# A graph network's third layer on TensorE: products by halves in its first block, and who mixes the features for them

## The chip, the cores and the metric

The kernel runs on one core of a Trainium2 chip. A core has five engines with an instruction queue each: TensorE (PE in the profile; its loading of weights is PEld), VectorE (DVE), ScalarE (ACT), GpSimd (POOL) and SyncE (SP, which here only starts DMAs). An engine takes its instructions in order and waits for semaphores of the others. The metric is the device time of one execution in microseconds; lower is better. Before the change it is 2798.02 us, the median of three runs (2794.73 to 2802.38).

## The reference

Four graph layers on 4096 nodes with 256 features; each adds its result to its input and normalises the rows. What matters here is the third layer (and the end of the second, whose last block is finished while the third begins):

```
def _L2_gnn_ref(x, adj, W, a):
    h = x @ W
    e_src = h @ a[:D, 0]
    e_dst = h @ a[D:, 0]
    e = e_src[:, None] + e_dst[None, :]
    e = jnp.where(e > 0, e, NEG_SLOPE * e)
    att_logits = jnp.where(adj > 0, e, MASK_VAL)
    attention = jax.nn.softmax(att_logits, axis=1)
    h_prime = attention @ h
    return jax.nn.elu(h_prime)
...
x = _layernorm(x + _L1_gnn_ref(x, adj, ...), axis=-1)
x = _layernorm(x + _L2_gnn_ref(x, adj, L2_gnn_W, L2_gnn_a), axis=-1)
```

All of it is float32.

## The kernel before

`additive_one` computes the third layer. The 4096 target nodes are taken in 8 blocks of 512 (`b`), the 4096 source nodes in 32 tiles of 128, two tiles to a pair (`g`, 16 pairs in a block). So there are 128 units (b, g). For each unit `weights(b, g)` makes the unnormalised attention weights: ScalarE an activation per tile into a PSUM bank (line 566, tile `r`, two banks), VectorE one operation per tile (line 567) that adds a term and multiplies by the mask, which SyncE loads (line 554, four buffers). The result is `prob`, 128 sources x 2 tiles x 512 targets. `sums(b, g)` multiplies it by the features of the sources, X, and adds up over all pairs in PSUM; W is applied afterwards, to the sums (`project`).

A pair can be multiplied in two ways. Plainly: four matmuls of 128 x 128 features with 512 targets (line 581), two banks in use. Or by Strassen's scheme on the 2 x 2 halves (two tiles, two halves of the features, two halves of the targets): seven products with 256 targets (`product`, line 446) in place of eight, on four banks `acc0` to `acc3`. The seven need sums and differences of the operands. Those of the weights, `mix`, come anew for each unit (`mix_weights`: line 436 on VectorE, 512 columns; lines 437 and 438 on GpSimd, 256 columns each). Those of the features, `mixed`, are made once for the layer, by `mix_features` for a group `q` of two pairs at a time (eight groups; four operations on lines 429 to 432). Before the change block 0 is multiplied plainly throughout, while VectorE makes the mixed features of all groups after each second pair; blocks 1 to 7 use the seven products. At the end of a block the four banks are combined into the four quarters of the result (`first_half`, `second_half`: lines 451 to 460); in block 0 three copies do (lines 589 to 591).

The order of the work is written out by hand for TensorE, VectorE and ScalarE: a loop over the units, in which `weights` runs three units ahead of `sums` (`LAG`). GpSimd and SyncE are ordered by a scheduler, within what the program fixes. In block 0 the loop also takes the steps of the second layer's tail (`next(before, None)`, with a number of steps for some pairs): it adds up the row sums `den` (line 867), row sums and transposes on TensorE (lines 880, 888, 895), divides and adds to X (909, 912), takes statistics (156, 157), the root (161 to 171, of which 168 to 171 and the lifting of the mean, 190 and 191, on GpSimd), scales the last four tiles of rows (186) and takes their dot products (504); then `factors` (511 to 513). Only after that can the weights of the last two pairs, 14 and 15, be made: their sources are these rows. `first_mask` holds the masks of pairs 0 and 1.

Of the kernel before, what the change touches and what calls it, by code (L numbers as in the profile page):

```python
# [9 lines left out]
FP = mybir.dt.float32  # L10
# [18 lines left out]
def kernel(  # L29
# [395 lines left out]

    def mix_features(t, q):

        x = X[:, 4 * q:4 * q + 4, :D].rearrange("p (g n) (h f) -> p g n h f", n=2, h=2)
        nc.vector.tensor_tensor(t[:, :, 0, :], x[:, :, 0, 1, :], x[:, :, 0, 0, :], OP.subtract)
        nc.vector.tensor_tensor(t[:, :, 1, :], x[:, :, 1, 1, :], t[:, :, 0, :], OP.add)  # L430
        nc.vector.scalar_tensor_tensor(t[:, :, 2, :], x[:, :, 1, 1, :], -1.0, x[:, :, 0, 1, :], OP.mult, OP.subtract)
        nc.vector.tensor_tensor(t[:, :, 3, :], x[:, :, 1, 0, :], t[:, :, 1, :], OP.subtract)

    def mix_weights(s, z, eng):

        nc.vector.tensor_tensor(s[:, :2, :], z[:, 0, :].rearrange("p (h i) -> p h i", h=2), z[:, :, HW:], OP.subtract)  # L436
        eng.tensor_tensor(s[:, 2, :], z[:, 0, :HW], s[:, 1, :], OP.subtract)
        eng.tensor_tensor(s[:, 3, :], z[:, 1, :HW], s[:, 2, :], OP.subtract)

    def product(acc, z, s, t, g, n):  # L440
# [5 lines left out]
        nc.tensor.matmul(acc[at][:, half * HW:(half + 1) * HW], w, a, start=(g == 0 and half == 0),  # L446
                         stop=(g == NP - 1), skip_group_check=True)

    def first_half(c, one, acc):
# [17 lines left out]
    class Additive:  # L467
# [38 lines left out]

        def factors(self, b):

            t = slice(b * QB, (b + 1) * QB)
            d = self.dot[:, t, 1]  # L510
            nc.scalar.activation(self.dst[:, t], d, AF.Exp)
            nc.scalar.activation(self.own[:, t], d, AF.Exp, scale=self.slope)
            nc.vector.tensor_scalar_mul(self.less[:, t], self.own[:, t], -1.0)

# [12 lines left out]
    def additive_one(w_sb, ga, tail, op, follow):  # L527

        with ExitStack() as lay:
# [13 lines left out]
            edges = adjT.rearrange("(t p) i -> p t i", p=P)  # L543
            mixed, acc, prob, mix, mvs, roots, kept, drawn, ys, far_y = {}, {}, {}, {}, {}, {}, {}, {}, {}, {}

            def bank():
                return ps.tile([P, QW], FP, name="g")

            def weights(b, g):
# [13 lines left out]
                for n in range(2):  # L563
# [3 lines left out]
                    nc.vector.scalar_tensor_tensor(z[:, n, :], r, ga.own[:, j:j + 1], mask[:, n, :], OP.add, OP.mult)  # L567
                if b:
                    s = mix[b, g] = zp.tile([P, 4, HW], FP, name="mix")
                    mix_weights(s, z, nc.gpsimd)  # L570

            def sums(b, g):
                if g == 0:
                    acc[b] = [pa.tile([P, QW], FP, name=f"acc{n}") for n in range(4)]
                if b:
                    for n in range(7):
                        product(acc[b], prob[b, g], mix[b, g], mixed[g // 2][:, g % 2], g, n)
                else:
                    for j in range(2 * g, 2 * g + 2):
                        for c in range(KC):  # L580
                            nc.tensor.matmul(acc[b][c], X[:, j, c * P:(c + 1) * P], prob[b, g][:, j % 2, :],
                                             start=(j == 0), stop=(j == NT - 1))
                if g == NP - 1:
                    c = kept[b] = op.tile([P, 4, HW], FP, name="quarters")
                    if b:
                        first_half(c, op.tile([P, HW], FP, name="one"), acc[b])
                        second_half(c, acc[b])
                    else:
                        nc.scalar.copy(c[:, :2, :], acc[b][0].rearrange("p (h i) -> p h i", h=2))
                        nc.vector.tensor_copy(c[:, 3, :], acc[b][1][:, :HW])  # L590
                        nc.vector.tensor_copy(c[:, 2, :], acc[b][1][:, HW:])

# [54 lines left out]
            fixed = {mybir.EngineType.PE, mybir.EngineType.DVE, mybir.EngineType.Activation}  # L647
            before = tail(bank)
            with tc.manual_schedule(engines=fixed):
                for i in range(len(units) + LAG):  # L650
                    b, g = units[i - LAG] if i >= LAG else (-1, 0)
                    if g == NP - 1:
                        sums(b, g)
                    if i < len(units):
                        weights(*units[i])
                    if b >= 0:
# [4 lines left out]
                        else:  # L661
                            for _ in range({4: 3, 6: 2, 7: 3, 8: 4, 9: 3, 10: 4}.get(g, 0)):
                                next(before, None)
                            if g == 11:
                                follow.start()
                            elif g == 14:
                                follow.centre(bank())
                            if g % 2:
                                t = mixed[g // 2] = keep.tile([P, 2, 4, P], FP, name=f"mixed{g // 2}")
                                mix_features(t, g // 2)  # L670
                        if b > 2 and g == 0:
# [19 lines left out]
    def multi_head_attention(w_sb, b_sb, tail, rows_of_den, rows_done, narrow_edges, ga):  # L691
# [290 lines left out]
        def tail(bank):  # L982
# [19 lines left out]
            yield  # L1002
            end_root(v, r, n, nc.gpsimd)
            lift_mean(mv, v, r, nc.gpsimd)
            yield
            for k in range(QB):
                scale_row(X[:, b * QB + k, :D], mv, r, k)
                ga.dots(b * QB + k, (1,))
                yield
            ga.factors(b)  # L1010
            rows_done()
# [375 lines left out]
```

## Time and profile before

| | us |
|---|---|
| median of three runs | 2798.02 |
| lowest and highest run | 2794.73, 2802.38 |
| the profiled execution: its own time | 2795.6 |
| its span in the profile | 2793.8 |
| block 0 of the third layer on TensorE | 1713.81 to 1772.03 |
| blocks 1 to 7 and the fourth layer | the rest, to 2793.8 |

The granted clock of TensorE is 1.0 in the profiled execution. In the profile, a line of the timeline gives the start, the length, the engine, the line of the kernel, what is written and read, how many instructions were merged, and in brackets how long the engine had been idle before and for whom it waited. A group of instructions gives its busy time, the mean duration in ns, and the idle time before it. Matmuls and weight loads have two records each. TensorE's matmuls overlap, so the pace is read from start to start.

### The profile page before, as it was taken

The page shows a single profiled execution, that of the slowest core. Times are in us where ns is not written, and L with a number is a line of the kernel's source. Part 1 is how long each engine was busy: PE and PEld are TensorE (multiplying, and loading weights), DVE is VectorE, ACT ScalarE, POOL GpSimd, SP SyncE. Part 2 cuts the span into 40 slices and gives each one's busy share as a digit, 9 for nine tenths or more (in the row PEclk, how much of TensorE's full clock was granted, in tenths as well). Part 3 has the DMA queues.
Part 4 walks back from the last instruction along what each step waited for, and adds up shares of the span by engine and source line. Part 5 has one row for each costly group of instructions (what it writes and reads, how often), then busy time and mean ns, then how long its engine had stood idle before and what let it go on. Part 6 is the DMA issues. An engine that isn't in the chain of part 4 may idle for free. (4 is left out here: it accounts for less than half of the span.)

```text
span 2793.8 us, 50176 instructions
## 1 busy us (share of the span) xinstructions
PE 2774.1 (99%) x19445; PEld 1427.4 (51%) x19445; DVE 2289.0 (82%) x3040; ACT 1700.7 (61%) x2650; POOL 1052.5 (38%) x986
## 2 busy tenths in 40 slices
PE   9999999999999999999999999999999999999999
PEld 5333333333453333333333333788888777777776
DVE  8899999999677788887888878888887877767676
ACT  7899999999336666666666666465556422222222
POOL 0000100100029878778788793345455000000000
PEclk9999999999999999999999999999999999999999
DMA  7566676665339899998988988567778545445442
GB/s 206 107 142 137 139 144 130 137 143 114 70 97 191 186 178 196 191 188 182 197 182 189 192 181 187 168 198 207 183 207 232 121 76 82 74 71 82 75 72 44
DMA packets 275065, 411.92 MB, mean 147 GB/s; under 512 B 54809, under 2 KB 155657, under 8 KB 273930
## 3 DMA queue, kind: packets, MB, share of 16 engines
q0 software_dynamic: 104176, 182.74, 41.3%
q1 hardware_dynamic: 164280, 218.88, 26.7%
q10 hardware_dynamic: 6370, 7.10, 0.7%
q8 instruction: 152, 2.49, 0.4%
q14 instruction: 87, 0.71, 0.1%
HBM read 335.94 MB, written 39.40 MB: 134 GB/s over the span
## 5 line engine op out<-in xcount | busy, mean ns | idle before, releaser
L834 DVE TENSOR_TENSOR prob<-p,mask 128x1024 f32<-128x1024 f32 x512 | 620.0, 1222 | 166.9 <-ACT p L824 159.9
L824 ACT ACTIVATE p<-p,shift 128x1024 f32<-128x1024 f32 x512 | 557.0, 1090 | 317.8 <-PE p L822 317.1
L312 PE MATMUL acc<-prob,V 128*32 128x512 f32 x6144 | 664.0, 592 | 1.2 <-DVE prob L302 1.2
L299 ACT ACTIVATE prob<-row,dst 128x512 f32<-128x512 f32 x1020 | 635.9, 716 | 0.4
L302 DVE SCALAR_TENSOR_TENSOR prob<-prob,mask 128x2048 f32<-128x2048 f32 x256 | 580.6, 2288 | 25.8 <-ACT prob L299 24.8
L844 POOL TENSOR_TENSOR den<-den,prob 128x1024 f32<-128x1024 f32 x220 | 559.8, 2544 | 92.6 <-DVE prob L834 87.2
L822 PE MATMUL p<-qT,kT 64*64 64x512 f32 x4096 | 531.1, 590 | 2.0 <-DVE prob L834 2.0
L858 PE MATMUL acc<-prob,V 64*64 64x512 f32 x4096 | 529.9, 589 | 0.0
L312 PEld LDWEIGHTS acc<-prob,V 128*32 128x32 f32 x6144 | 197.3, 110 | 453.0 <-issue 432.2
L446 PE MATMUL acc<-mix,mixed 128*128 128x256 f32 x1428 | 388.0, 380 | 2.7 <-DVE quarters L460 1.2
L858 PEld LDWEIGHTS acc<-prob,V 64*64 64x64 f32 x4096 | 157.4, 133 | 282.1 <-issue 280.3
L822 PEld LDWEIGHTS p<-qT,kT 64*64 64x64 f32 x4096 | 154.3, 133 | 278.9 <-issue 256.5
L446 PEld LDWEIGHTS acc<-mix,mixed 128*128 128x128 f32 x1428 | 269.5, 190 | 45.0 <-PE acc L446 3.5
L90 POOL COPY tick<-prob 128x1 f32<-128x1 f32 x35 | 38.0, 1086 | 643.0 <-DVE prob L302 642.1
L1130 DVE TENSOR_TENSOR prob<-prob,mask 128x1024 f32<-128x1024 f32 x128 | 156.2, 1220 | 140.5 <-ACT prob L1122 140.1
L850 POOL DMA_DIRECT2D den<-prob x240 | 232.0, 967 | 61.0 <-DVE prob L834 22.3
L446 PE MATMUL acc<-prob,X 128*128 128x256 f32 x952 | 245.7, 380 | 3.4 <-DVE quarters L452 3.3
L1050 POOL DMA_DIRECT2D mask<-in_adjT x64 | 47.7, 745 | 530.1 <-DVE prob L1130 437.6
L446 PEld LDWEIGHTS acc<-prob,X 128*128 128x128 f32 x952 | 180.1, 190 | 84.1 <-issue 56.7
L567 DVE SCALAR_TENSOR_TENSOR prob<-r,own,mask 128x512 f32<-128x512 f32 x252 | 177.1, 744 | 51.3 <-POOL s L169 13.7
L1122 ACT ACTIVATE prob<-p 128x512 f32<-128x512 f32 x144 | 86.1, 598 | 204.1 <-PE p L1118 202.6
L1122 ACT ACTIVATE prob<-g 128x512 f32<-128x512 f32 x112 | 67.0, 598 | 208.7 <-PE g L1118 208.7
(233 smaller groups left out, 2823.1 us busy)
## 6 DMA issues: line engine op xcount, KB each, us to landing
mask<-in_adjT SPq DMA_DIRECT2D x254, 512.0 KB
den<-prob POOLq DMA_DIRECT2D x240, 512.0 KB, 5.3
mask<-edges SPq DMA_DIRECT2D x512, 64.0 KB
mask<-in_adjT POOLq DMA_DIRECT2D x64, 512.0 KB, 5.7
edges<-in_adj POOLq DMA_DIRECT2D x32, 512.0 KB, 9.6
far<-squares SPq DMA_DIRECT2D x16, 512.0 KB
den<-prob SPq DMA_DIRECT2D x16, 512.0 KB
row<-far SPq DMA_DIRECT2D x7, 1024.0 KB
```

Of the source, the lines that this page charges most:

```text
L299: nc.scalar.activation(z[:, h, :], r, AF.Relu, bias=-1.0, scale=dst[:, j, h:h + 1])
L302: nc.vector.scalar_tensor_tensor(z, z, 1.0, mask[m][:, j % MJ, :].unsqueeze(1).to_broadcast([P, H, QW]), OP.add, OP.mult)
L312: nc.tensor.matmul(acc[b][h * G:(h + 1) * G, n, :], part, prob[b, j][:, h, :], start=(j == 0), stop=(j == NT - 1))
L446: nc.tensor.matmul(acc[at][:, half * HW:(half + 1) * HW], w, a, start=(g == 0 and half == 0), stop=(g == NP - 1), skip_group_check=True)
L567: nc.vector.scalar_tensor_tensor(z[:, n, :], r, ga.own[:, j:j + 1], mask[:, n, :], OP.add, OP.mult)
L822: nc.tensor.matmul(p[c * d:(c + 1) * d, r, :], kT[half, c, at:at + d], qT[half, c, cols], start=True, stop=True)
L824: nc.scalar.activation(p, p, AF.Exp, bias=shift)
L834: nc.vector.tensor_tensor(z, p, mask[m][:, j % MJ, :].unsqueeze(1).to_broadcast([P, KC, QW]), OP.mult)
L844: nc.gpsimd.tensor_tensor(to, to, flat, OP.add)
L850: nc.gpsimd.dma_start(to, flat, accum_op=OP.add)
L858: nc.tensor.matmul(acc[b][c][r * d:(r + 1) * d, :], V[half, j, r * d:(r + 1) * d], prob[b, j][half, r, :], start=(j == 0), stop=(j == NH - 1))
L1130: nc.vector.tensor_tensor(z, z, co.mask[b, 2 * g // MJ][:, lo:lo + 2, :], OP.mult)
```

## The change

In block 0, pairs 4 to 13 (`apart`) are now multiplied by the seven products, and pairs 0 to 3, 14 and 15 by eight plain products of 256 targets onto the same four banks (`plain`), so that the end of the block combines the banks as in the other blocks; what the plain products put into the second half of `acc3` is copied apart and added at last (`more`). The mixed features are made earlier and in another order: groups 0, 1 and 2 on VectorE, groups 3 to 7 on GpSimd, but for one operation of each group, which stays on VectorE. The table `mixing` says at which step each group is made. From step 16 on a group's mixing is placed after the last operation that `weights` gave to GpSimd (`last`). The small operations of the tail's root and mean go from GpSimd to VectorE, the multiplication by -1 in `factors` (`less`) from VectorE to ScalarE, and one step of the tail comes a little earlier.

```diff
-    def mix_features(t, q):
+    def mix_features(t, q, eng=nc.vector):
         x = X[:, 4 * q:4 * q + 4, :D].rearrange("p (g n) (h f) -> p g n h f", n=2, h=2)
-        nc.vector.tensor_tensor(t[:, :, 0, :], x[:, :, 0, 1, :], x[:, :, 0, 0, :], OP.subtract)
-        nc.vector.tensor_tensor(t[:, :, 1, :], x[:, :, 1, 1, :], t[:, :, 0, :], OP.add)
+        eng.tensor_tensor(t[:, :, 0, :], x[:, :, 0, 1, :], x[:, :, 0, 0, :], OP.subtract)
+        eng.tensor_tensor(t[:, :, 1, :], x[:, :, 1, 1, :], t[:, :, 0, :], OP.add)
         nc.vector.scalar_tensor_tensor(t[:, :, 2, :], x[:, :, 1, 1, :], -1.0, x[:, :, 0, 1, :], OP.mult, OP.subtract)
-        nc.vector.tensor_tensor(t[:, :, 3, :], x[:, :, 1, 0, :], t[:, :, 1, :], OP.subtract)
+        eng.tensor_tensor(t[:, :, 3, :], x[:, :, 1, 0, :], t[:, :, 1, :], OP.subtract)
...
+    def plain(acc, z, g):
+        for at, to, f, lo in ((0, 0, 0, 0), (1, 1, 1, 0), (2, 1, 0, HW), (3, 1, 1, HW)):
+            for n in range(2):
+                nc.tensor.matmul(acc[at][:, to * HW:(to + 1) * HW], X[:, 2 * g + n, f * P:(f + 1) * P],
+                                 z[:, n, lo:lo + HW], start=(g == 0 and n == 0), stop=(g == NP - 1),
+                                 skip_group_check=True)
...
-        def factors(self, b):
+        def factors(self, b, times=nc.vector.tensor_scalar_mul):
...
-            nc.vector.tensor_scalar_mul(self.less[:, t], self.own[:, t], -1.0)
+            times(self.less[:, t], self.own[:, t], -1.0)
...
+            apart = range(4, 14)
+            mixing = {1: ((2, nc.vector),), 2: ((3, nc.gpsimd), (4, nc.gpsimd)), 3: ((5, nc.gpsimd),),
+                      4: ((0, nc.vector), (6, nc.gpsimd)), 14: ((1, nc.vector),), 16: ((7, nc.gpsimd),)}
...
-                if b:
+                if b or g in apart:
                     s = mix[b, g] = zp.tile([P, 4, HW], FP, name="mix")
-                    mix_weights(s, z, nc.gpsimd)
+                    return mix_weights(s, z, nc.gpsimd)
...
-                if b:
+                if (b, g) in mix:
                     for n in range(7):
                         product(acc[b], prob[b, g], mix[b, g], mixed[g // 2][:, g % 2], g, n)
                 else:
-                    for j in range(2 * g, 2 * g + 2):
-                        for c in range(KC):
-                            nc.tensor.matmul(acc[b][c], X[:, j, c * P:(c + 1) * P], prob[b, g][:, j % 2, :],
-                                             start=(j == 0), stop=(j == NT - 1))
+                    plain(acc[b], prob[b, g], g)
                 if g == NP - 1:
                     c = kept[b] = op.tile([P, 4, HW], FP, name="quarters")
-                    if b:
-                        first_half(c, op.tile([P, HW], FP, name="one"), acc[b])
-                        second_half(c, acc[b])
-                    else:
-                        nc.scalar.copy(c[:, :2, :], acc[b][0].rearrange("p (h i) -> p h i", h=2))
-                        nc.vector.tensor_copy(c[:, 3, :], acc[b][1][:, :HW])
-                        nc.vector.tensor_copy(c[:, 2, :], acc[b][1][:, HW:])
+                    if b == 0:
+                        more = fin1.tile([P, QW], FP, name=f"kept{KC}")[:, :HW]
+                        nc.scalar.copy(more, acc[b][3][:, HW:])
+                    one = op.tile([P, HW], FP, name="one")
+                    first_half(c, one, acc[b])
+                    second_half(c, acc[b])
+                    if b == 0:
+                        nc.vector.tensor_tensor(c[:, 2, :], c[:, 2, :], more, OP.add)
...
+                    for q, eng in mixing.get(i, ()):
+                        t = mixed[q] = keep.tile([P, 2, 4, P], FP, name=f"mixed{q}")
+                        with tc.issue_after(getattr(last, "ins", last)) if i >= NP else nullcontext():
+                            mix_features(t, q, eng)
                     if i < len(units):
-                        weights(*units[i])
+                        last = weights(*units[i]) or last
...
-                            for _ in range({4: 3, 6: 2, 7: 3, 8: 4, 9: 3, 10: 4}.get(g, 0)):
+                            for _ in range({4: 3, 6: 2, 7: 3, 8: 5, 9: 3, 10: 3}.get(g, 0)):
...
-                            if g % 2:
-                                t = mixed[g // 2] = keep.tile([P, 2, 4, P], FP, name=f"mixed{g // 2}")
-                                mix_features(t, g // 2)
...
-            end_root(v, r, n, nc.gpsimd)
-            lift_mean(mv, v, r, nc.gpsimd)
+            end_root(v, r, n)
+            lift_mean(mv, v, r)
...
-            ga.factors(b)
+            ga.factors(b, nc.scalar.mul)
```

## The prediction

> **What bounds the kernel now.** I read the page first, for the engine that sets the end, then the stage of the change: the third layer's first block, about 1713.8 to 1772.0 us. The page's first part:
>
> ```profile
> PE 2774.1 (99%) x19445; PEld 1427.4 (51%) x19445; DVE 2289.0 (82%) x3040; ACT 1700.7 (61%) x2650; POOL 1052.5 (38%) x986
> ```
>
> The view of busy time in a stretch (its length, then each engine's busy time, TensorE's clock, the DMA share and GB/s):
>
> ```profile
> 1713.00:1773.00 60.00, 59.97 (x173) 27.40 (x166) 48.67 (x105) 29.39 (x46) 4.52 (x10) 1.00 0.68 189
> ```
>
> TensorE has no gap, so fewer products save time as long as nothing else is late. VectorE is busy for 48.67 of 60 us; GpSimd is almost idle. The groups of this stage:
>
> ```profile
> L581 PE MATMUL acc<-prob,X 128*128 128x512 f32 x128 | 55.8, 594 | 0.0
> L567 DVE SCALAR_TENSOR_TENSOR prob<-r,own,mask 128x512 f32<-128x512 f32 x36 | 25.5, 746 | 5.7 <-DMA mask<-in_adjT 4.3 <-ACT r L566 1.0
> ...
> L432 DVE TENSOR_TENSOR mixed<-X,mixed 128x256 f32<-128x256 f32 x8 | 3.3, 416 | 0.0
> ...
> L437 POOL TENSOR_TENSOR mix<-prob,mix 128x256 f32<-128x256 f32 x3 | 2.3, 782 | 18.8 <-PE g L1041 14.2 <-DVE mix L436 4.6
> ...
> L436 DVE TENSOR_TENSOR mix<-prob 128x512 f32<-128x512 f32 x3 | 2.1, 692 | 0.1
> ```
>
> The trace holds two records for each matmul, so x128 is 64 matmuls. Next the timelines, for pace and for who is late. TensorE, at the block's end and in the next block:
>
> ```profile
> 1743.69 24.20 PE L581 MATMUL acc<-prob,X 128*128 128x512 f32 x56
> 1767.73 1.03 PE L1041 MATMUL g<-w_sb,ones 128*128 128x256 f32 x4
> 1768.59 3.60 PE L581 MATMUL acc<-prob,X 128*128 128x512 f32 x8
> 1772.03 1.03 PE L446 MATMUL acc<-prob,X 128*128 128x256 f32 x4
> ...
> 1774.55 0.67 PE L446 MATMUL acc<-mix,mixed 128*128 128x256 f32 x2 [1.07 <-DVE quarters L591]
> ```
>
> VectorE's holes in the stage, and two of its operations that ran beside GpSimd's L437 and L438:
>
> ```profile
> 1724.62 1.41 DVE L567 SCALAR_TENSOR_TENSOR prob<-r,own,mask 128x512 f32<-128x512 f32 x2 [3.90 <-DMA mask<-in_adjT]
> ...
> 1754.58 0.41 DVE L186 TENSOR_SCALAR X<-X,mv,r 128x256 f32<-128x256 f32 x1 [2.25 <-POOL mv L191]
> ...
> 1762.02 1.46 DVE L567 SCALAR_TENSOR_TENSOR prob<-r,own,mask 128x512 f32<-128x512 f32 x2 [0.85 <-ACT r L566]
> ...
> 1769.00 0.83 DVE L430 TENSOR_TENSOR mixed<-X,mixed 128x256 f32<-128x256 f32 x1
> 1769.75 0.94 DVE L431 SCALAR_TENSOR_TENSOR mixed<-X 128x256 f32<-128x256 f32 x1
> ```
>
> Two things to see. The weights of pair 14 are written from 1762.02 to about 1763.4, and TensorE reaches pair 14 near 1764.4 (1767.73 less one pair of 3.45): only 1.0 us of slack, because pair 14 uses rows that the second layer's tail finishes in this very stage. And L430 and L431, 0.42 us alone, took 0.83 and 0.94 us while GpSimd worked.
>
> **What the Trainium skill says.** "SBUF — State Buffer", section "SBUF: two separate sides": a VectorE operation with two SBUF inputs and a GpSimd operation that reads SBUF exclude each other for the whole instruction, the later one waits. The two doubled rows agree; L567 (one input in PSUM) stays at 0.74 beside GpSimd. "GPSIMD Engine Reference", section "8. Key points": elementwise work is about twice as fast on VectorE; here 0.73 to 0.78 us against 0.42 for 256 columns.
>
> **The change part by part,** against the profiled execution (span 2793.8, run 2795.6 us).
>
> TensorE. A pair of four 512-column matmuls takes 24.04/7 = 3.43 us in the second stretch and 24.23/7 = 3.46 in the first, 3.45 in the mean. In the next block three pairs of seven products go from 1807.03 to 1816.09: 3.02 each, 0.431 a product. Ten pairs save 10 x 0.43 = 4.3 us. The six plain pairs become eight products of 256, 8 x 0.431 = 3.45: nothing. Freed of all waits, pair 14 would start at 1759.9 and the block end at 1767.7.
>
> VectorE. Added: ten L436 (0.61 us from start to start, 6.1) and six small operations of the tail's root and mean, which leave GpSimd (0.16 each and a dependence, 0.19: 1.1). Removed: of the 24 mixing operations of this stage 7 (the four operations for each of six groups of two pairs become four for groups 0 to 2 and one for groups 3 to 7; 0.36 each, 2.5) and `less`, to ScalarE (0.2). Net +4.5 us: about 53.2 of a stage that wants to shrink to 55.7, so VectorE nearly fills it. I walk its new order, with 2.05 us for a pair with L436 (1781.16 to 1783.21 in the next block) and 0.35 for a dot product:
> - Pairs 0 to 3: the mixing of group 2 (1.46) falls into the 1.67 us before pair 1; the single operations of groups 3 to 6 and all of group 0 (1.4 + 1.46 = 2.9) fall into the 3.90 us before the mask of pair 4. Pair 4 is ready at 1726.0, as before. If all these alternate with GpSimd's twelve mixing operations, at some 0.8 us each, 0.8 later.
> - Pairs 5 to 7 with dots: mix of 4 at 1726.6, + 3 x 2.40, + 2.45 for the two sums of den = 1736.3. TensorE wants den at 1727.65 + 3 x 3.02 = 1736.7. With contention (GpSimd gets in between the two 1.2 us sums, 0.7, and the 0.8 of the start) 1737.5 to 1737.8: TensorE waits about 1.
> - Pairs 8 to 10: 6.2 and 0.5 for ScalarE behind the row sums, 1743.0; halves 3.1, 1746.1 (1745.95 before, so the earlier transposes win nothing); pair 11 2.05; four statistics 2.15; `v` at 1750.3.
> - ScalarE's root 0.5, and the activation of pair 12 now queued behind it 0.8, with hand-offs 1.5 idle; pair 12 2.05; six small operations 1.1; two rows scaled and dotted 1.6; pair 13 2.05; two rows more 1.6: 1760.3. Before: 1760.6.
> - Factors 0.6, activation 0.8, two L567: pair 14 ready at 1763.2. The mixing of group 1 is covered by these 1.4 us; where it alternates with GpSimd's group 7 it lasts some 3 instead of 1.46 and adds 1.5.
> So the chain through the tail is as long as before, and TensorE, ahead by 4.3, runs into it. Its first matmuls of pair 14 start with the first half of pair 14, 1762.7; + 3.75 for the pair, 0.86 for the centring product, 3.46 = 1770.8, a gain of 1.25 on 1772.03. With contention everywhere (0.8 + 0.3 + 1.5) 1773.3, a loss of 1.25.
>
> Moved mixing on GpSimd: 15 operations of 0.73 plus twenty of the weights, 25.6 us in an engine with 4.5 busy; its DMA issues are over at 1714.8. The last two of pair 4's weights end 1728.3 to 1729.2; TensorE wants them at 1728.5 and 1729.4: hidden, with 0.2 to spare.
>
> The change of blocks. Before, the first pair of the next block takes 1772.03 to 1776.35, 4.32, which is 1.30 over 3.02. After, two copies of 0.35 on ScalarE stand before VectorE's chain (at the next boundary 1824.74, 1825.52, 1825.98, 1826.50, 1827.22: 2.9 us), and the third bank is free at its end: 1.6 to 1.8 over. +0.35. SyncE: one weight load goes before a mask, read 20 us later: nothing. Groups 6 and 7 leave the next block's VectorE, which has slack there: nothing.
>
> Sum: -1.25 to +1.25, +0.35: -0.9 to +1.6, middle +0.35. The runs' median is 2798.02, 2.4 above the profiled run, so 2798.3.
>
> **Rivals.**
> - All the gain arrives: -4.3 + 0.35, 2794.1. For it: TensorE is full and GpSimd free. Against: pair 14 would have to be ready by 1759.9, over 3 us earlier than in the walk.
> - Slower: the shared read stretches VectorE's chain. Place: from the den sums to pair 14. Price: each two-input operation that meets GpSimd +0.4; 4 dots behind the weights of pairs 12 and 13 (1.6), L436 in three pairs (0.8), on top of 1.25: +3.7 with the boundary, 2801.7. It decides once the last dot product of the tail ends after about 1761.5. For it: 0.83 and 0.94. Against: in the next block most L436 are at 0.69, since GpSimd is done by then.
>
> **How the numbers follow.** Forecast 0.55, full gain 0.17, slower 0.28. Single runs of before lie from 2794.73 to 2802.38, so each case gets some 2.5 us either side: 2792 to 2804 holds eight in ten. 0.3% (8.4 us) is about what a measurement tells from no change; even the full gain is half of it. Faster by more 0.05, slower by more 0.09 (some stall that I do not see), within it 0.86.
>
> **What would show it.** Right: seven products at 3.02 a pair, then a TensorE gap at pair 14 (and 13) put down to VectorE's prob; VectorE with hardly a hole from 1726 on; mixing operations of 0.8 to 0.9 beside GpSimd. Wrong: no gap at pairs 12 to 14 (then full gain), or gaps on `mix` of GpSimd in every pair (then a loss beyond mine).

## The result, and the profile after

| | before | after |
|---|---|---|
| median of six runs each (us) | 2795.84 | 2807.45 |
| lowest and highest run | 2794.73, 2802.38 | 2802.79, 2809.19 |
| the profiled execution: its own time, its span | 2795.6, 2793.8 | 2802.79, 2801.0 |
| mean granted clock of TensorE in it | 1.000 | 0.998 |

The kernel before has three runs more here than ahead of the change. The ratio after to before is 1.0036, 95% interval 1.0027 to 1.0046, which is some 10 us; the medians lie 11.6 us apart. The forecast was 2798.3 with a range of 2792 to 2804. The time lies outside the range, on the slow side; to a slowing by more than 0.3% the prediction had given 0.09.

Line numbers have moved: the weights are now L578 (L567 before), the activations L577, the plain products L453 (L581 before), den sums L877, reciprocals L913, dot products L512. The mixing of features keeps L429 to L432, the sums of the weights L436 to L438. The page's first part of the changed kernel:

```profile
PE 2773.3 (99%) x19553; PEld 1450.0 (52%) x19553; DVE 2302.6 (82%) x3044; ACT 1697.6 (61%) x2652; POOL 1077.5 (38%) x1015
```

Nothing is to be seen there. The shares are those of before to a per cent, because the stage is 2% of the span. The same 60 us that the prediction looked at, in the view of busy time in a stretch (length, then PE, PEld, DVE, ACT, POOL, TensorE's clock, DMA share, GB/s):

```profile
1713.00:1773.00 60.00, 49.31 (x231) 41.20 (x231) 56.42 (x99) 23.82 (x39) 26.60 (x35) 0.92 0.60 154
```

TensorE, with no gap before, now stands idle for 10.7 of the 60 us, and its mean clock is 0.92; VectorE went from 48.67 to 56.42. The timeline of all engines at the start of the block shows the greater part of it at one place:

```profile
1711.32 1.05 POOL L860 DMA_DIRECT2D den<-prob  x1
1711.42 3.32 PEld L453 LDWEIGHTS acc<-prob,X 128*128 128x128 f32 x16 [0.81 <-issue]
1711.42 3.72 PE L453 MATMUL acc<-prob,X 128*128 128x256 f32 x16
...
1711.58 9.25 DVE L429 TENSOR_TENSOR mixed<-X 128x256 f32<-128x256 f32 x1
1711.91 1.89 POOL L429 TENSOR_TENSOR mixed<-X 128x256 f32<-128x256 f32 x2
...
1718.74 1.80 POOL L432 TENSOR_TENSOR mixed<-X,mixed 128x256 f32<-128x256 f32 x2
1720.86 0.42 DVE L430 TENSOR_TENSOR mixed<-X,mixed 128x256 f32<-128x256 f32 x1
...
1721.88 1.40 DVE L578 SCALAR_TENSOR_TENSOR prob<-r,own,first_mask 128x512 f32<-128x512 f32 x2
```

VectorE's first mixing operation, 0.42 us alone, lasts 9.25 us. It starts at 1711.58, while GpSimd still issues a DMA (1711.32 to 1712.37 by its record, which runs on beside the next operation). From 1711.91 GpSimd goes through its twelve mixing operations without a pause, one about every 0.68 us, to 1720.54; VectorE's operation ends 0.3 us after that. The next one is back at 0.42. Behind it, in the same queue, stand the weights of pair 1, which TensorE wanted at 1714.9 and gets at 1722.67. TensorE's timeline, all of its gaps up to the second block:

```profile
1722.67 12.28 PE L453 MATMUL acc<-prob,X 128*128 128x256 f32 x48 [7.53 <-DVE prob L578]
1765.94 1.13 PE L446 MATMUL acc<-mix,mixed 128*128 128x256 f32 x4 [0.61 <-POOL mix L437]
1770.88 5.16 PE L453 MATMUL acc<-prob,X 128*128 128x256 f32 x16 [2.51 <-DVE prob L578]
1781.10 1.42 PE L446 MATMUL acc<-prob,X 128*128 128x256 f32 x4 [0.74 <-ACT one L459]
```

And the clock after two of these gaps, in the view of stretches:

```profile
1715.00:1722.60 7.60, 0.14 (x1) 0.00 (x0) 7.57 (x6) 0.00 (x0) 5.54 (x9) 0.78 0.87 232
1722.60:1725.00 2.40, 2.33 (x6) 1.83 (x7) 2.40 (x6) 1.84 (x3) 0.00 (x0) 0.50 0.04 7
1725.00:1728.00 3.00, 3.00 (x13) 2.59 (x12) 2.97 (x8) 2.61 (x4) 0.00 (x0) 0.83 0.53 139
...
1771.00:1776.00 5.00, 5.00 (x17) 4.13 (x18) 4.72 (x8) 4.32 (x6) 0.33 (x1) 0.72 0.54 163
```

After the long gap TensorE works at half its clock for over 2 us. Pairs 1 to 3 take 12.12 us (1722.67 to 1734.79) instead of 3 x 3.45 = 10.35.

From the start of block 0 to the second pair of the next block: before 1713.81 to 1776.35, 62.54 us; after 1711.42 to 1785.01, 73.59. The 11.05 more are made up so: ten pairs of seven products -4.3; the gap ahead of pair 1 +7.8; the clock in pairs 1 to 3 +1.8; pair 13 +0.9 (0.61 of it the gap); the gap ahead of pair 14 +2.6; pair 14 at the lowered clock +1.55; change of blocks +0.5: +10.9. (The profiled execution of after is the fastest of its six, its block 0 happens to begin 2.4 us earlier than the one of before, and what follows is 1.5 us shorter, so the spans are only 7.2 apart.)

### The profile page after: what moved, and what is told of

Same layout as the page of the kernel before. It is cut to its first block, busy times and chain, and to the rows that moved or that the text cites. A ratio compares the mean times of both kernels' runs of the same rounds, so it can differ in the third digit from the quotient of the medians.

```text
span 2801.0 us, 50446 instructions
## 1 busy us (share of the span) xinstructions
PE 2773.3 (99%) x19553; PEld 1450.0 (52%) x19553; DVE 2302.6 (82%) x3044; ACT 1697.6 (61%) x2652; POOL 1077.5 (38%) x1015
## 3 DMA queue, kind: packets, MB, share of 16 engines
q8 instruction: 153, 2.51, 0.4%
## 5 line engine op out<-in xcount | busy, mean ns | idle before, releaser
L446 PE MATMUL acc<-mix,mixed 128*128 128x256 f32 x1488 | 403.8, 380 | 1.5 <-DVE quarters L468 0.8
L446 PEld LDWEIGHTS acc<-mix,mixed 128*128 128x128 f32 x1488 | 281.1, 190 | 44.4 <-PE acc L446 2.3
L446 PE MATMUL acc<-prob,X 128*128 128x256 f32 x992 | 256.4, 380 | 4.4 <-DVE quarters L460 3.6
L446 PEld LDWEIGHTS acc<-prob,X 128*128 128x128 f32 x992 | 187.5, 190 | 86.8 <-issue 56.6
L578 DVE SCALAR_TENSOR_TENSOR prob<-r,own,mask 128x512 f32<-128x512 f32 x252 | 176.9, 743 | 47.1 <-POOL mix L437 11.7
```

## The experiments

The question after the result was whether the long operation is a wait for GpSimd's run, and what keeps VectorE out for all of it, where the prediction had the two take turns. The second was what the change costs once this wait is gone. Each ratio below is to the kernel before, run beside it.

**GpSimd's operations one after another.** Groups 3 to 6 are mixed in sequence, so that nearly every GpSimd operation needs the one before it; the operations are the same. (In the part of the diff that is not shown, `mix_features` returns its last operation and `chain` starts as None.)

```diff
-                        with tc.issue_after(getattr(last, "ins", last)) if i >= NP else nullcontext():
-                            mix_features(t, q, eng)
+                        after = last if i >= NP else chain
+                        with tc.issue_after(getattr(after, "ins", after)) if after is not None and eng is nc.gpsimd else nullcontext():
+                            done = mix_features(t, q, eng)
+                        if eng is nc.gpsimd:
+                            chain = done
```

> The changed kernel, but GpSimd makes groups 3 to 6 one after another, so that each of its operations waits for the one before it; in the changed kernel two groups alternate and the twelve run without a pause. Starvation (a run of GpSimd operations without a pause keeps the shared read from a VectorE operation with two SBUF inputs until the run ends): VectorE's first mixing operation takes at most about 1 us in place of 9.25, TensorE's gap of 7.5 us before pair 1 goes, and the time falls by 8 to 10 us to within 3 us of the kernel before (ratio 0.999 to 1.001). Rival (the DMA traffic of that moment, or GpSimd as such, holds VectorE): the operation still takes 8 to 9 us and the ratio stays at 1.003 to 1.004.

Measured: 2799.64 us, ratio 1.0009 [1.0001, 1.0018]. VectorE's timeline, then GpSimd's:

```profile
1712.51 1.81 DVE L429 TENSOR_TENSOR mixed<-X 128x256 f32<-128x256 f32 x1
1714.35 0.83 DVE L430 TENSOR_TENSOR mixed<-X,mixed 128x256 f32<-128x256 f32 x1
1715.11 0.94 DVE L431 SCALAR_TENSOR_TENSOR mixed<-X 128x256 f32<-128x256 f32 x1
```

```profile
1712.84 1.19 POOL L429 TENSOR_TENSOR mixed<-X 128x256 f32<-128x256 f32 x1
1714.11 0.80 POOL L430 TENSOR_TENSOR mixed<-X,mixed 128x256 f32<-128x256 f32 x1
1714.98 0.79 POOL L432 TENSOR_TENSOR mixed<-X,mixed 128x256 f32<-128x256 f32 x1
```

Between 1712.84 + 1.19 = 1714.03 and 1714.11 GpSimd now pauses for 0.08 us, waiting for its own result, and VectorE is let in at the first of these pauses: 1.81 us instead of 9.25 (about 1 had been expected), then turns of 0.83 to 0.94. Its first operation starts 0.33 us ahead of GpSimd's (1712.51 and 1712.84), as in the changed kernel. This is what the prediction had expected of the change itself. The gap ahead of pair 1 falls from 7.53 to 1.57 us, and 8 us of the loss are gone, with the same operations on the same engines.

**All mixing on VectorE.** GpSimd mixes nothing.

```diff
-            mixing = {1: ((2, nc.vector),), 2: ((3, nc.gpsimd), (4, nc.gpsimd)), 3: ((5, nc.gpsimd),),
-                      4: ((0, nc.vector), (6, nc.gpsimd)), 14: ((1, nc.vector),), 16: ((7, nc.gpsimd),)}
+            mixing = {1: ((2, nc.vector),), 2: ((3, nc.vector), (4, nc.vector)), 3: ((5, nc.vector),),
+                      4: ((0, nc.vector), (6, nc.vector)), 14: ((1, nc.vector),), 16: ((7, nc.vector),)}
```

> The changed kernel with all mixing on VectorE, at the same steps; the seven products stay. Starvation: no mixing operation over 0.5 us near pairs 0 to 4, no TensorE gap before pair 1. VectorE has 15 more operations, 5.4 us; those before pair 4 do not all fit into its wait for the mask, so pairs 13 and 14 come 2 to 5 us later than with the work on GpSimd: ratio 1.000 to 1.002. Rival (DMA traffic): the first mixing operation is still long, ratio 1.003 or more.

Measured: 2799.56 us, ratio 1.0011 [1.0002, 1.0019]. VectorE's timeline, then GpSimd's:

```profile
1714.53 0.41 DVE L429 TENSOR_TENSOR mixed<-X 128x256 f32<-128x256 f32 x1
```

```profile
1714.26 1.04 POOL L860 DMA_DIRECT2D den<-prob  x1
```

The operation that had lasted 9.25 us again starts while the same DMA is issued, and with no run behind it takes 0.41: the DMA issue alone does not hold it. Every mixing operation takes 0.41 to 0.43 us and nothing waits ahead of pair 1, though VectorE has fifteen operations more. TensorE's gaps come later: 0.94 us on GpSimd's sum for pair 4, 0.68 on den, 1.93 on the reciprocals, 0.35 ahead of pair 14.

**GpSimd's run kept, VectorE's own mixing behind it.** Groups 2 and 0, and the single operations of groups 3 to 6, come after the weights of pair 3. In the diff `mix_third` is the operation of L431 as a function of its own; for groups 1 and 7, and in the fourth layer, it follows `mix_features` directly.

```diff
-            mixing = {1: ((2, nc.vector),), 2: ((3, nc.gpsimd), (4, nc.gpsimd)), 3: ((5, nc.gpsimd),),
-                      4: ((0, nc.vector), (6, nc.gpsimd)), 14: ((1, nc.vector),), 16: ((7, nc.gpsimd),)}
+            mixing = {2: ((3, nc.gpsimd), (4, nc.gpsimd)), 3: ((5, nc.gpsimd),),
+                      4: ((6, nc.gpsimd), (2, nc.vector), (0, nc.vector)), 14: ((1, nc.vector),), 16: ((7, nc.gpsimd),)}
...
+                    if i == 4:
+                        for q in (2, 3, 4, 5, 6, 0):
+                            mix_third(mixed[q], q)
```

> The changed kernel with GpSimd's run of twelve kept as it is, but VectorE's own mixing (groups 2 and 0, and the third operation of groups 3 to 6) put behind the weights of pair 3, so that beside the run VectorE has only operations with one input in PSUM. Starvation of two-input operations alone: the weights of pairs 1 to 3 come at 0.7 us an operation during the run, TensorE has no gap before pair 1, and VectorE's first mixing operation waits at most for the rest of the run, 0 to 3 us; ratio 0.999 to 1.001. Rival (GpSimd's run or DMA traffic holds every VectorE operation): the weights of pair 1 are late by some 8 us, ratio 1.003 or more.

Measured: 2800.86 us, ratio 1.0015 [1.0008, 1.0021]. The weights of pairs 1 to 3, which VectorE makes during the unbroken run, take their usual 1.40 to 1.45 us for two: one of their inputs, `r`, lies in PSUM. So the run does not hold every operation of VectorE. The ratio is above the 0.999 to 1.001 expected: TensorE now waits 0.60 us ahead of pair 4, 0.94 on GpSimd's sum for it, 0.68 on den, 1.93 on the reciprocals and 1.70 ahead of pair 14.

**The hold by itself.** A small kernel that has one VectorE operation at a time beside runs of GpSimd operations of 128x256. Each duration is from one execution.

> A small kernel by itself, which only copies x to its output and leaves the whole computation out: GpSimd runs k additions of 128x256, free of each other or each on the result of the one before, and one VectorE operation of 128x256 starts when the run has begun. Starvation: with two SBUF inputs it takes about 0.4 us + 0.7 us for each free GpSimd operation (k = 12: 8 to 9 us), and at most 1.3 us beside a run of dependent ones whatever its length; with one input in PSUM, or one input alone, about 0.4 us throughout. Rival (one operation waits for at most one other): 1.2 us at most in every case. Rival (DMA traffic): 0.4 us in every case, as no DMA runs here.

Measured, VectorE's timeline, three of its twelve operations (the name says: inputs, whether GpSimd's operations are free of each other or a chain, and how many):

```profile
28.46 0.93 DVE L42 TENSOR_TENSOR two_free_twelve<-a,b 128x256 f32<-128x256 f32 x1 [4.82 <-POOL b L34]
...
49.85 0.42 DVE L46 TENSOR_TENSOR psum_free_twelve<-q,b 128x256 f32<-128x256 f32 x1 [8.74 <-POOL b L34]
58.14 8.27 DVE L44 TENSOR_SCALAR one_free_twelve<-b 128x256 f32<-128x256 f32 x1 [7.86 <-POOL b L34]
```

GpSimd's run beside the last of them:

```profile
58.06 8.20 POOL L38 TENSOR_TENSOR one_free_twelve_run<-e,c 128x256 f32<-128x256 f32 x12
```

With two SBUF inputs it waited for one GpSimd operation only, 0.93 us, however long the run was (0.92 to 1.00 for 1 to 12): the expectation of a wait as long as the run failed for this case. With one input in PSUM it never waited. But an operation with a single SBUF input was held for all 8.27 us of the run, and for 0.79 only beside the chain. It started 0.08 us behind the run's first operation, without any DMA; so did the two-input one at 28.46, behind a run that began at 28.38. So a hold as long as an unbroken run exists, and whether it comes was not settled by the number of inputs.

**When the operation starts.** The same, with the kernel's access pattern, its order of GpSimd operations, a DMA issue ahead of the run, and later starts.

> A kernel of its own that copies x to the output and leaves all of the reference's computation out; only the durations of single VectorE instructions count. It repeats the earlier probe with the kernel's own access pattern (two strided halves of 128 of the feature rows), with GpSimd's twelve operations in the kernel's order (two groups interleaved, each operation waiting for the one two before it), and with the VectorE operation started either with the run (bare), during a GpSimd DMA issue ahead of it (dma), or some time into it, behind a VectorE operation on PSUM of 32 to 256 columns. Theory A (the hold comes from starting before or at the edge of an unbroken run, whatever the pattern): the dma cases last 8 us or more, the bare ones 0.9 or 8, the shifted ones about 0.9. Theory B (the strided pattern or the interleaving keeps VectorE out): all mix cases beside pairs or loose last 6 us or more, the flat ones 0.9. Theory C (VectorE is always let in after one operation, and the 9.25 us of the changed kernel are something else): 0.8 to 1.3 us everywhere for the two-input ones. The one-input case beside the flat run was 8.27 us; if it is due to the form of the operation it is 8 again.

Measured, VectorE's timeline, nine of its operations:

```profile
25.49 1.02 DVE L79 SCALAR_TENSOR_TENSOR two_flat_dma<-a,mark,b 128x256 f32<-128x256 f32 x1 [7.54 <-POOL mark L52]
34.73 0.93 DVE L72 SCALAR_TENSOR_TENSOR mix_pairs_bare<-X,mark 128x256 f32<-128x256 f32 x1 [8.22 <-POOL mark L52]
43.20 0.48 DVE L72 SCALAR_TENSOR_TENSOR mix_pairs_dma<-X,mark 128x256 f32<-128x256 f32 x1 [7.54 <-POOL mark L52]
...
61.37 1.52 DVE L72 SCALAR_TENSOR_TENSOR mix_loose_dma<-X,mark 128x256 f32<-128x256 f32 x1 [8.38 <-POOL mark L52]
...
71.44 8.81 DVE L74 TENSOR_TENSOR mix_pairs_dma<-X 128x256 f32<-128x256 f32 x1
...
80.74 0.72 DVE L74 TENSOR_TENSOR mix_pairs_bare<-X 128x256 f32<-128x256 f32 x1
...
97.87 0.52 DVE L74 TENSOR_TENSOR mix_pairs_bare<-X 128x256 f32<-128x256 f32 x1
...
114.27 8.86 DVE L77 TENSOR_SCALAR one_pairs_dma<-b,mark 128x256 f32<-128x256 f32 x1 [7.54 <-POOL mark L52]
...
123.67 0.52 DVE L77 TENSOR_SCALAR one_pairs_bare<-b,mark 128x256 f32<-128x256 f32 x1
```

GpSimd's timeline around the one of 71.44:

```profile
71.18 0.57 POOL L54 DMA_DIRECT2D den<-X  x1
71.77 1.41 POOL L40 TENSOR_TENSOR mixes<-X 128x256 f32<-128x256 f32 x2
...
78.58 1.39 POOL L44 TENSOR_TENSOR mixes<-X,mixes 128x256 f32<-128x256 f32 x2
```

The pattern doesn't decide (mix cases of 0.52 to 0.93), nor does the number of inputs (one-input cases of 0.52 and 8.86). What the long ones share here is a start ahead of the run, during the DMA issue: 71.44 is 0.33 us ahead of the run's first operation, and 114.27 is 0.50 (that run began at 114.77). In the changed kernel it is 1711.58 against 1711.91, again 0.33. An operation that starts some way into the run (80.74, 97.87, 123.67; 0.28 to 0.48 us behind its beginning) is let in after the GpSimd operation under way. Not every start during the DMA issue is held: 43.20 was done before the run began, and 25.49 and 61.37 lasted 1.02 and 1.52 us. Nor is such a start the only way into a hold: the 8.27 us of the first probe began 0.08 us behind the run's first operation, and four operations here that began with the run or up to 0.08 us behind it lasted only 0.79 to 1.00. A one-input operation beside the same kind of run took 0.53 when it began 0.34 us into it. Theory A was right in kind, not in saying that all such cases are held.

**The hold without the seven products.** Of ten pairs only pair 13 keeps them; everything else is as changed.

```diff
-            apart = range(4, 14)
+            apart = (13,)
```

> The changed kernel with one edit: of its ten pairs of seven products only pair 13 keeps them, pairs 4 to 12 are plain. GpSimd's run of twelve mixing operations and VectorE's mixing stay as changed. Theory A (the unbroken run holds VectorE's first mixing operation and that is the loss): the operation still lasts 8 us or more, TensorE waits over 7 us ahead of pair 1 and works at a lowered clock after it: 2805 to 2807, as slow as the whole change. Theory B (the loss comes from the seven-product pairs, their sums on VectorE and GpSimd): back to 2797 or less.

Measured: 2804.69 us, ratio 1.0026 [1.0016, 1.0037]. VectorE's timeline, then TensorE's:

```profile
1714.34 9.24 DVE L429 TENSOR_TENSOR mixed<-X 128x256 f32<-128x256 f32 x1
```

```profile
1725.42 23.23 PE L453 MATMUL acc<-prob,X 128*128 128x256 f32 x96 [7.53 <-DVE prob L578]
```

The hold is there to 0.01 us, and with it 8.5 of the 11.6 us (by the medians; the intervals of the two ratios overlap, so the split is rough). There is no gap at pairs 13 and 14: these come only with the ten pairs of seven products, to which what is left of the 11.6 us is put down.

**The run started later.** GpSimd's run stays unbroken, but begins behind VectorE's mixing of group 2.

```diff
+                        if i == 1:
+                            for n in (3, 4, 5, 6):
+                                mixed[n] = keep.tile([P, 2, 4, P], FP, name=f"mixed{n}")
+                                nc.vector.tensor_copy(mixed[n][:, 0, 0, :1], t[:, 0, 3, :1])
```

> The changed kernel with GpSimd's run of twelve kept as it is, but started only behind VectorE's mixing of group 2: VectorE writes one column of the tiles of groups 3 to 6 after that mixing (four copies of 128x1), and GpSimd's first operations wait for them. Theory A (a hold as long as the run meets a VectorE operation that has begun just before the run does; one that comes later is let in after an operation of GpSimd): the first mixing operation takes 0.4 to 1.1 us instead of 9.25, the two or three mixing operations that VectorE still has in mid-run 0.8 to 1.3 each, no gap over 1 us ahead of pair 1, and a time like that of the experiments without the hold: 2799.0 to 2801.0. Theory B (any two-input VectorE operation on SBUF beside the run is held to its end): the hold moves to the first mixing operation after pair 1's weights, some 6 to 7 us there, and a gap of some 4 us ahead of pair 2 or 3: 2803 to 2806.

Measured: 2798.28 us beside 2797.64 of the kernel before in the same comparison, ratio 1.0005 [0.9996, 1.0013]. VectorE's timeline:

```profile
1713.19 0.41 DVE L429 TENSOR_TENSOR mixed<-X 128x256 f32<-128x256 f32 x1
...
1720.98 0.83 DVE L430 TENSOR_TENSOR mixed<-X,mixed 128x256 f32<-128x256 f32 x1
1721.74 0.94 DVE L431 SCALAR_TENSOR_TENSOR mixed<-X 128x256 f32<-128x256 f32 x1
```

The first mixing operation is at 0.41, those in mid-run take 0.41 to 0.94, and there is no gap ahead of pair 1. Beside the changed kernel the run begins behind group 2 (at 1715.07, where GpSimd's DMA issue began at 1712.92) and VectorE has four small copies more, 0.34 us together; the ratio falls from 1.0036 to 1.0005. The time is a little under what was expected. As the run no longer follows the DMA issue directly, this doesn't show which of the two, the order of the starts or the issue just ahead, brings the hold about.

**What is left without the hold: load or chain?** In the first three kernels without the hold 3.3 to 4.6 us remain (in the last one 0.6, with an interval that reaches to 3.6), with gaps at the reciprocals and ahead of pair 14. In the next kernel (on top of the chained GpSimd operations) VectorE's mixing of groups 0 and 1 goes behind the weights of pair 15:

```diff
-                      4: ((0, nc.vector), (6, nc.gpsimd)), 14: ((1, nc.vector),), 16: ((7, nc.gpsimd),)}
+                      4: ((6, nc.gpsimd),), 16: ((0, nc.vector), (7, nc.gpsimd)), 17: ((1, nc.vector),)}
```

> GpSimd's mixing as a chain with gaps, as in the first experiment, and in addition VectorE's mixing of groups 0 and 1 moved out of the first block: both are first needed in the second block, and come behind pair 15's weights instead of ahead of pairs 4's and 14's. Theory A (with the hold gone VectorE, with next to no idle time from the mask product to pair 14, is what bounds the block, so what stands on it ahead of pair 14's weights counts in full): pair 14 comes 2.4 us earlier for group 1 and up to 2 for group 0, the gaps of 2.51 and 1.65 us shrink to under 0.5 each, 2796.0 us, ratio 0.9995 to 1.0003 to the kernel before. Theory B (the chain of the tail, not VectorE's load, ends last): group 0 gives nothing, group 1 gives 2.4 at most: 2797.5. Theory C (the rest of the loss lies at the change of blocks or after): 2799.5, unchanged from the first experiment.

Measured: 2799.05 us, ratio 1.0011 [1.0004, 1.0018]. The gap at the reciprocals went from 1.65 to 0.32 us, as theory A said, but the one ahead of pair 14 only from 2.51 to 1.69, and the time is that of theory C, unchanged from the first experiment. VectorE's timeline shows why:

```profile
1761.00 0.83 DVE L512 CUSTOM_DVE_ANT_0 kept<-X,a_row 128x256 f32<-128x256 f32 x1
1761.77 0.08 DVE L512 DVE_READ_ACCUMULATOR2_ANT dot<- 128x1 f32 x1
1763.32 1.41 DVE L578 SCALAR_TENSOR_TENSOR prob<-r,own,mask 128x512 f32<-128x512 f32 x2 [1.48 <-POOL mixed L432]
```

Where the mixing stood, VectorE now waits for 1.48 us. (The releaser named is GpSimd's; the weights need the factors and the activation that ScalarE makes from the last dot product.) The mixing of group 1 had filled this wait. And the next block's first pair paid for the rest: 2.16 us of waiting for the quarters, behind the moved mixing, and a clock of 0.57 in the 3 us after it.

The same with the six steps of the tail two pairs earlier:

```diff
-                            for _ in range({4: 3, 6: 2, 7: 3, 8: 5, 9: 3, 10: 3}.get(g, 0)):
+                            for _ in range({2: 3, 4: 2, 5: 3, 6: 5, 7: 3, 8: 3}.get(g, 0)):
```

> The same, with all six steps of the previous layer's tail two pairs earlier. Theory A (VectorE's load bounds the block): the tail ahead of time displaces pairs' weights instead, and no more than 1 us is won over the kernel without this: 2795 to 2796. Theory B (the tail's chain from the turned rows to pair 14 ends last): pair 14 never waits, and TensorE's saving of 4.3 us comes out but for the change of blocks: 2792.5 to 2793.5, ratio 0.9987 to 0.999.

Measured: 2799.33 us, ratio 1.0010 [1.0002, 1.0018]. Pair 14 no longer waits, as theory B said; but TensorE waits 2.53 us at the reciprocals instead, works at a clock of 0.50 for the 2 us behind this gap, and waits 0.32 and 0.89 in pair 13. The tail ahead of time displaced the weights of the pairs, as theory A said, and even the last microsecond that A had left for it did not come.

**Fewer pairs of seven products.** On top of the chained GpSimd operations: six pairs (8 to 13), groups 2, 3 and 0 on VectorE at pairs 4 to 6, groups 4 to 6 chained on GpSimd, the tail one pair earlier; then the same with the tail where the change has it; then eight pairs (6 to 13) with the earlier tail.

```diff
-            apart = range(4, 14)
+            apart = range(8, 14)
...
-                            for _ in range({4: 3, 6: 2, 7: 3, 8: 5, 9: 3, 10: 3}.get(g, 0)):
+                            for _ in range({3: 3, 5: 2, 6: 3, 7: 5, 8: 3, 9: 3}.get(g, 0)):
```

> Seven products for pairs 8 to 13 only (six instead of ten); GpSimd mixes groups 4, 5, 6 and 7, one operation after another; VectorE mixes groups 2, 3 and 0 behind pairs 3 to 5 and group 1 ahead of pair 14; the tail's steps one pair earlier. Theory A (VectorE's load, 50.8 of 62.2 us before and 58.4 of 63.9 in the first experiment, takes up TensorE's saving): VectorE has six times 0.69 for the sums and loses about as much mixing to GpSimd, so it stays near 51 us, TensorE never waits over 0.5 us in the block, and six times 0.43 less 0.4 at the change of blocks come out: 2794.0 us, ratio 0.9988 to 0.9996. Theory B (the seven-product form costs TensorE itself its saving through GpSimd's last sum, which comes late for a pair): about 2796.5 with waits on GpSimd's mix.

> The same with the tail's steps where the changed kernel has them. Theory A (load): the same time as with the earlier steps, within 0.5 us. Theory C (the chain from the turned rows to pair 14 ends last): a gap of 0.8 to 1.8 us ahead of pair 14, and so much longer than with the earlier steps.

> Seven products for pairs 6 to 13 (eight); GpSimd mixes groups 3 to 6 and 7, VectorE groups 2 and 0 behind pairs 3 and 4, group 1 ahead of pair 14; tail's steps one pair earlier. Theory A: VectorE near 52 us, hardly more than before; eight times 0.43 less 0.4 and some 0.5 to 1 of new waits: 2793.5 to 2794.5. Theory B: waits on GpSimd's mix for each pair in which VectorE runs late: 2797.

Measured: 2797.43 us, 1.0002 [0.9994, 1.0011]; 2797.51 us, 1.0002 [0.9994, 1.0010]; 2798.91 us, 1.0009 [1.0001, 1.0017]. The gains that the first and the third were to bring did not come, though the waits on GpSimd's sums that their theory B named stayed under 1 us; the second took the same time as the first, as its theory A said. The gaps move with the tail, and the time does not: with the earlier tail 1.48 us at the reciprocals and 1.15 + 0.94 at pair 13, with the later one 2.51 ahead of pair 14. VectorE's load shows in one stretch, from the weights of pair 0 to the end of those of pair 14, for the kernel before, then for ten pairs without the hold (the first experiment), then for six pairs with the earlier tail, one fence for each:

```profile
1712.60:1763.50 50.90, 50.87 (x151) 22.62 (x148) 39.90 (x90) 24.26 (x39) 3.35 (x8) 1.00 0.69 193
```

```profile
1711.10:1766.60 55.50, 49.29 (x246) 40.50 (x243) 53.02 (x100) 24.35 (x40) 30.75 (x37) 0.99 0.66 177
```

```profile
1711.80:1767.10 55.30, 51.32 (x255) 41.61 (x251) 48.49 (x99) 24.19 (x40) 20.53 (x26) 1.00 0.66 177
```

VectorE's busy time is the fourth number: 39.90, 53.02 and 48.49 us. With ten pairs it has more to do up to pair 14 than the kernel before takes for all of it (50.9 us), so in that order of work TensorE's saving cannot show. With six pairs its work would fit, by the total; what it lacks is slack at the places where the tail's chain runs. So load alone does not explain the six-pair kernels: there, by the places of the gaps, it is the chain of VectorE, ScalarE and TensorE steps from the den sums to pair 14, with the pairs' weights in between, and at which pair its wait appears is a matter of placement. This is argued, not shown, and how load and chain share the rest was not separated further. No version tried was faster than the kernel before.

## Why the prediction was wrong

- *TensorE, a pair of seven products in 3.02 us.* Right: 1749.19 to 1764.30 for five pairs, 3.02 each.
- *Pairs 0 to 3: the mixing of group 2 falls into 1.67 us; "if all these alternate with GpSimd's twelve mixing operations, at some 0.8 us each, 0.8 later".* This is the step that failed. It was mis-sized by an order of magnitude: they did not alternate, and pair 1 came 7.8 us late, with 1.8 more for TensorE's clock behind it. Taken away in four ways (GpSimd chained, no GpSimd mixing, VectorE's mixing later, GpSimd's run later), the time falls to 1.0005 to 1.0015 of the kernel before; put alone, it makes 1.0026. The prediction drew on the Trainium skill, "SBUF — State Buffer", section "SBUF: two separate sides", for an exclusive pair of ports that is kept for the whole instruction. The runs agree with this for one instruction (0.83 to 0.94 us). They differ in who waits: the prediction had the later one wait, but in the changed kernel VectorE's operation starts 0.33 us before the run's first, by the profile, and still ends behind the whole run; here the measurement decides. That the loser gets its turn at the next instruction was the prediction's own addition; it holds against a GpSimd that pauses, and against a run that VectorE meets in the middle, but not always at a run's start.
- *VectorE +4.5 us.* Too small. In the stretch just shown it is 53.02 - 39.90 = +13.1 us without the hold. Contention with GpSimd is some 7.5 of it, summed from the first experiment's timeline: 2.8 for the mixing of group 2 (1.81, 0.83, 0.94, 0.94 instead of 0.42 each), 1.8 for the other mixing, 0.9 for two small operations of the root (0.59 and 0.58 instead of 0.16 each), 0.8 for two dot products (0.83 instead of 0.42 each), 0.4 for a scaling (0.80 instead of 0.41), 0.4 for the den sums (2.88 instead of 2.48) and 0.35 for two L436. The other 5.6 are near the forecast, as of the mixing taken away only a part stood in this stretch. The prediction had up to 2.6 for all contention, and half of that in the middle of its sum.
- *The chain through the tail as long as before or up to 2.6 longer, and TensorE runs into it at pair 14.* Right in place, too short in size: from the reciprocals to the weights of pair 14 it was 19.2 us before (1742.80 to 1762.02) and 21.8 after (1748.30 to 1770.09), 21.65 in the first experiment. That is 2.6 longer in this part alone, where the forecast had at most 1.5; its other 1.1 stood ahead of the reciprocals. The gap came at pair 14 (2.51) and 13 (0.61), as the last part said it would. That it lowers TensorE's clock, 1.55 us more in pair 14, was not in the sum.
- *den wait about 1, transposes win nothing.* Hidden in the changed kernel, since TensorE was late; without the hold none or 0.68 for den and 1.65 to 1.93 at the reciprocals (the first three experiments), which had been costed as nothing.
- *GpSimd's last sum of pair 4 hidden with 0.2 to spare.* In the changed kernel hidden; with all mixing on VectorE 0.94 us late, since VectorE was.
- *Change of blocks +0.35.* Right: 0.74 idle and 3.91 for the first pair are 4.65 against 4.32, +0.3; with what lies between pair 15 and the gap +0.5.
- *The rivals.* The slower one (a stretched VectorE chain from the den sums to pair 14, +3.7) comes near what remains without the hold, +3.3 us in the first two experiments, but partly by chance: of its terms only two of the four dot products and two of the three L436 came, and with the 0.35 of the boundary they add up to 4.0, not 3.7. It missed the hold, which is another mechanism at another place. The full gain was far off.

## What to carry to other kernels

Where GpSimd is given a run of elementwise work on SBUF, look at what VectorE does around the run's start, from half a microsecond ahead of it: an operation there can be held to the end of the run, and everything queued behind it with it. Give VectorE's operation a head start by a dependence, let GpSimd's operations depend on each other so that it pauses, or put VectorE operations with an input in PSUM there. And where a full engine is relieved at the cost of the next fullest, price the work on that one with the stretching it suffers, up to the point of the chain where it is first needed.

## What the runs showed that was not expected

- A VectorE operation of 0.42 us lasted 9.25, 9.24 and 8.81 us beside a GpSimd run without pauses that began 0.33 us after it, and an operation with one SBUF input 8.27 and 8.86 us (begun 0.08 us behind and 0.50 ahead of the run's first operation). With pauses of 0.08 us between GpSimd's operations the same start led to 1.81 us, and the one-input operation took 0.79. Whether a start at the run's edge is held is not settled: of the five operations of the second probe that began during a DMA issue, two were. What GpSimd's DMA issue has to do with it is open: the 8.27 us came without one, and where GpSimd mixes nothing the same start takes 0.41.
- With one input in PSUM, operations next to such a run kept their times (0.42 in the probe; 1.40 to 1.45 for two of the weights).
- A gap on TensorE can cost more than itself. Behind 7.53 us the clock was 0.50 for 2.4 us and 0.83 in the next 3, 1.8 us lost in all. The Trainium skill, "TensorE: Matmul & The Clock Gate", section "Part 1: The HAM clock gate", tells of half the clock after an idle window of some 3.4 us; here shorter gaps were followed by a lowered clock too. Behind 2.51 us it was 0.72 over the next 5 us (pair 14 took 5.0 us instead of 3.45), and it was lowered behind each of the seven gaps of 2.16 to 2.67 us that the kernels above have in block 0 and at its end. Behind 1.69 us pair 14 ran at its usual pace (a row of 3.95 us, in the kernel with groups 0 and 1 moved, against 5.16 here). In between both happened: behind 1.93 us at the reciprocals the clock was 0.72 (all mixing on VectorE) and 0.70 (VectorE's mixing later) in the next 2 us, behind 1.92 us (the run started later) it was 1.00. What decides there is open.
